# The x_proj matmuls of a Mamba-like block as two column tiles of one PSUM bank

## The chip, the core and the metric

The kernel runs on one core of a Trainium2 chip. The metric is the device time of one execution in microseconds (us), lower is better. All arithmetic is fp32.

## What is computed

The input x has shape (8, 384, 32, 32). Two layers follow one another, each with a group norm ahead of it and x added behind it. The first is a state-space (Mamba) block with an MLP, the second a mixture of four experts of which two are weighted per pixel. Cut to what matters here, the first layer is:

```python
t = layernorm(t)                                # (8, 1024, 384)
xm, z = split(t @ in_proj_w.T)                  # 768 channels each
xc = silu(causal_conv3(xm) + conv_b)
dbc = xc @ x_proj_w.T                           # 768 -> 24 + 16 + 16
dt, Bm, Cm = split(dbc, [24, 40])
dt = softplus(dt @ dt_proj_w.T + dt_proj_b)
h[l] = exp(dt * A) * h[l-1] + dt * xc * Bm      # 16 states per channel
y = (sum(h * Cm) + xc * D) * silu(z)
t = y @ out_proj_w.T;  t = gelu(t @ w1.T + b1) @ w2.T + b2
```

`dbc`, the product of `xc` with `x_proj_w`, is what the change is about: 56 numbers per token out of 768.

## The kernel before

Tokens are cut into 16 chunks (`NCH`) of 512 (`T`), two for each of the eight images. Channels lie on the 128 partitions: 384 are three blocks (`J`), 768 are six (`ND`). The 16 states are worked on as 4 steps (`NG`) of 4 states (`Q`), so a chunk takes 6 x 4 = 24 rounds, and the scan part of the kernel runs 384 rounds.

The backbone of a round is written out by hand in the loop over `rounds`: GpSimd multiplies dt * xc by B (`drive`, L738), ScalarE makes the four decays exp(dt * A) (`decay`, L730), VectorE runs four scans along the tokens (`scan`, L746), VectorE and GpSimd multiply by C (`read_out`, L750), and TensorE sums the states with four matmuls that lie beside one another in four column tiles of 32 (`sum_states`, L772). Decays, scans and read-out hand over to one another in both directions: the decays write PSUM tiles that the scans and the read-out have to leave first.

All other work is written as generators, called tasks: the next chunk's norm, input projection with convolution, gate, `x_proj` and `delta` (the dt projection), and for earlier chunks the output projection, both MLP layers and the first layer of the experts. A task yields the engine that its next step needs, a cost in us, and after how many slots it may go on. Three times in a round (`side`, a third of a round each) the engines get credit (TensorE 2.7, VectorE 0.6, ScalarE 2.7, 1.8 and 0.7), and `issue` lets the most urgent steps whose time has come go on while the credit lasts. A step that yields `"bank"` also needs one of four PSUM banks (`ps_g`), which `bank` takes and `free` gives back. All this happens while the program is built: on the chip every engine works off a fixed order, and instructions wait for one another by semaphores. A changed cost or wait of one task can therefore change the order of everything behind it. `plan` says in which round of a chunk the next chunk's tasks begin: convolutions in rounds 5 to 10, `x_proj` in round 11, the first `delta` in round 17, the loads of B and C (L374) from round 20 on.

`x_proj` (L361) is six matmuls, one for each block of 128 channels, that accumulate into 56 partitions of one bank. Each needs its block of `xc`, and these are finished in two batches of three by `silus` (L349). Then ScalarE copies the sum to SBUF (`dbc`, L366), and the SP queue writes the 32 rows of B and C to DRAM (`bc_dram`, L369), from where `load_b` and `load_c` fetch them spread over the partitions. The 24 rows of dt go into the matmul of `delta` (L399).

Ahead of the rounds, chunk 0 is prepared alone: its six convolutions with `x_proj(0)` and then its first `delta` stand in the open. After the rounds the pipeline of the MLP and the experts is drained, and the experts' second layer (L940) runs with no scan beside it.

Of the kernel before, what the change touches and what calls it, by code (L numbers as in the profile page):

```python
# [11 lines left out]
F32 = mybir.dt.float32  # L12
AF = mybir.ActivationFunctionType
ALU = mybir.AluOpType
# [4 lines left out]
P = 128  # L19
B, C, L = 8, 384, 1024  # L20
T = 512
# [4 lines left out]
ND = DI // P  # L26
# [11 lines left out]
DTR = 24  # L38
# [72 lines left out]
def layers(ctx, tc, io, ident, cmean, eps, dram, x1_dram, gn1, logits, r_dram, group_norm):  # L111
# [6 lines left out]
    nc = tc.nc  # L118
    V, S, G, PE = nc.vector, nc.scalar, nc.gpsimd, nc.tensor

    def pool(name, bufs, stack=ctx, **kw):
        return stack.enter_context(tc.tile_pool(name=name, bufs=bufs, **kw))
# [6 lines left out]
    p1, pdt, pxt, pdu = (pool(name, bufs, scanning)  # L129
                         for name, bufs in (("p1", 1), ("pdt", 2), ("pxt", NH), ("pdu", 3)))  # L130
# [16 lines left out]
    def weight(name, shape, queue=S):  # L147
        t = wp.tile(shape, F32, name="w_" + name)
        queue.dma_start(t, io[name])
        return t  # L150
# [5 lines left out]
    w_x = weight("x_proj", [P, ND, DTR + 2 * NS])  # L156
# [33 lines left out]
    xc, zs, dtr, dxr, dbc, bc_dram, bt, ct, gn = {}, {}, {}, {}, {}, {}, {}, {}, {}  # L190
# [8 lines left out]
    def bank(name):  # L199
        held[0] += 1  # L200
        return ps_g.tile([P, T], F32, name=name, tag="g")

    def free():
        held[0] -= 1
# [148 lines left out]
    def x_proj(i):  # L353
        g = None
        m = DTR + 2 * NS
        for d in range(ND):
            while (i, d) not in xc:
                yield "-", 0, 1
            yield "bank" if d == 0 else "PE", 1, 1 if d % 3 == 0 else 0
            g = bank("g_x") if d == 0 else g  # L360
            PE.matmul(g[0:m, :], lhsT=w_x[:, d, :], rhs=xc[i, d], start=(d == 0), stop=(d == ND - 1))  # L361
        yield "ACT", 0.6, 2
        while i > 0 and (i - 1, ND - 1) not in projected:
            yield "-", 0, 1
        dbc[i] = p1.tile([m, T], F32, name="dbc")
        S.copy(dbc[i], g[0:m, :])  # L366
        free()
        bc_dram[i] = dram.tile([2 * NS, T], F32, name=f"bc_dram{i}")
        nc.sync.dma_start(bc_dram[i], dbc[i][DTR:m, :])  # L369

    def load_rows(name, i, first):
        t = pbc.tile([P, T], F32, name=name)
# [346 lines left out]
    def at(r):  # L719
        i, k = divmod(r, per)  # L720
        return i, *divmod(k, NG)
# [75 lines left out]
    def behind_act():  # L797

        return 2 if now[0] == 2 else 1
# [23 lines left out]
    def plan(i, k):  # L823
# [8 lines left out]
        if n < NCH:  # L832
            if 5 <= k < 11:
                begin(conv(n, k - 5))
            if k in (7, 10):
                begin(silus(xc, accs, [(n, k - 7 + d) for d in range(3)]))
            if k in (11, 12, 13):
                begin(gate(n, k - 11))
            if k == 11:
                begin(x_proj(n))  # L840
            if k == 13:
                begin(silus(zs, gates, [(n, d) for d in range(3)]))
            if k == 17:
                begin(delta(n, 0), rank=0)
            if k == 21:
                begin(delta(n, 1), rank=0)
            if k >= per - NG:
                load_b(n, k - (per - NG))
            if k > per - NG:
                load_c(n, k - (per - NG) - 1)  # L850
# [97 lines left out]
    with tc.manual_schedule():  # L948
# [4 lines left out]
        drain()  # L953
        S.preload_act_table_set(SILU_SET)
        begin(*(conv(0, d, at_once=True) for d in range(ND)), x_proj(0))
        drain(lambda: len(xc) == ND)
        exp_ln_tables()
# [46 lines left out]
        for r in range(rounds):  # L1004
            i, d, s = at(r)
            k = r % per
# [74 lines left out]
```

## Time and profile before

| | us |
|---|---|
| median of 3 runs | 3979.28 (3975.89 to 3981.76) |
| the profiled execution | 3978.56 |
| its span, first to last instruction | 3976.8 |
| x_proj matmuls L361, 192 records | 97.7 busy |
| ScalarE's copy L366, 16 records | 9.2 busy, 575 ns each |
| VectorE's add from PSUM and SBUF L529, 48 records, 128x512 | 32.4 busy, 676 ns each |
| first to last round | about 72 to 3274 |
| experts' second layer, from about 3480 | 497.5 busy in L940 |

How to read it. PE is TensorE's matmul, PEld its weight load, DVE is VectorE, ACT ScalarE, POOL GpSimd, SP the queue from which most DMAs are issued. TensorE does an fp32 matmul in two passes, and the trace has a record for each: 192 records are 16 chunks of six matmuls. Passes overlap at their ends (a record lasts some 0.6 us where the next one starts 0.43 us later), so the distance from start to start is the measure of what one costs. The chain of waits is followed back from the last instruction, at each step to what released it; in a window it shows what set the pace there. A digit of the slices is the busy share of a fortieth of the span, in tenths.

### The profile page before, as it was taken

To read this page: it belongs to the slowest core of one execution; us is meant where nothing else is said; L and a number is where in the kernel's file an instruction comes from. 1 tells how busy PE (TensorE), PEld (TensorE's weight loads), DVE (VectorE), ACT (ScalarE), POOL (GpSimd) and SP (SyncE) were. 2 spreads that over 40 slices of the span, in tenths; PEclk is the share of its full clock that TensorE was granted. 3 is DMA by queue.
4 is the path that set the end of the run, shared out by engine and by line. 5 is a ranking of instruction groups with operands and counts; after the bars stand their busy time and mean duration, and the time that the engine had idled before them with its cause. 6 is when DMAs were issued, how large, how long until landed. Compare 5 with 4: busy or idle time off the path is not lost.

```text
span 3976.8 us, 35106 instructions
## 1 busy us (share of the span) xinstructions
PE 3654.0 (92%) x10294; PEld 1379.6 (35%) x10294; DVE 3029.6 (76%) x3081; ACT 2388.2 (60%) x3714; POOL 2780.9 (70%) x1070
## 2 busy tenths in 40 slices
PE   6679898999899989998999999999998998799999
PEld 2123232333333333333333333333333333344444
DVE  4988998888888888888888888888887771155554
ACT  4758676867686768676877677767777753100000
POOL 3998999788878888888888888888888870000000
PEclk8879898999999999999999999999999999899999
DMA  4444444465546554555555556554555553555552
GB/s 128 133 144 145 158 147 165 156 212 171 182 161 208 172 175 161 200 173 177 173 195 177 181 167 202 178 183 163 174 178 170 181 170 99 199 191 181 198 185 106
DMA packets 374803, 677.89 MB, mean 170 GB/s; under 512 B 40508, under 2 KB 151484, under 8 KB 372436
## 3 DMA queue, kind: packets, MB, share of 16 engines
q1 hardware_dynamic: 344800, 624.97, 47.3%
q10 hardware_dynamic: 29812, 50.68, 3.4%
q8 instruction: 82, 1.34, 0.1%
q14 instruction: 109, 0.89, 0.1%
HBM read 535.90 MB, written 139.59 MB: 170 GB/s over the span
## 4 chain that ended last, share of the span: by engine, by line
PE 58%; ACT 19%; DVE 14%; DMA 5%; issue 4%; SPq 1%; POOL 0%; ACTq 0%; DVEq 0%; POOLq 0%
PE acc L940 13%; PE acc L522 9%; PE g_in L298 8%; PE hid L483 7%; PE e_hid L618 7%; PE y L772 5%; PE g_out L461 5%; DVE da_A L746 4%; ACT da_A L730 4%; DVE du L746 4%; ACT da_B L730 2%; DMA r_dram<-r 2%; PE g_dt L399 2%; PE g_x L361 2%; ACT L194 2%
## 5 line engine op out<-in xcount | busy, mean ns | idle before, releaser
L738 POOL TENSOR_TENSOR du<-dxr,b 128x2048 f32<-128x2048 f32 x384 | 1738.7, 4528 | 29.4 <-PE y L772 18.4
L750 POOL TENSOR_TENSOR du<-du,c 128x1024 f32<-128x1024 f32 x384 | 906.3, 2360 | 235.3 <-DVE du L746 205.6
L730 ACT ACTIVATE da_B<-dtr_b,w_a_log 128x512 f32<-128x512 f32 x768 | 527.2, 686 | 404.1 <-DVE du L746 360.9
L730 ACT ACTIVATE da_A<-dtr_a,w_a_log 128x512 f32<-128x512 f32 x768 | 528.6, 688 | 245.4 <-DVE carry L755 120.2
L298 PE MATMUL g_in<-xt,in_proj 128*128 128x512 f32 x1152 | 559.4, 625 | 34.4 <-ACT edge L315 11.3
L618 PE MATMUL e_hid<-xn,e_w 128*128 128x512 f32 x1152 | 536.5, 611 | 40.9 <-DMA xn<-xn_dram 20.5
L746 DVE TENSOR_TENSOR_SCAN du<-da_B,carry,du 128x512 f32<-128x512 f32 x384 | 488.4, 1272 | 100.8 <-ACT da_B L730 100.0
L772 PE MATMUL y<-du,sel 128*32 128x512 f32 x3072 | 451.6, 631 | 120.1 <-DVE du L750 76.9
L483 PE MATMUL hid<-tt,mlp_w 128*128 128x512 f32 x1152 | 533.1, 603 | 21.0 <-ACT h L487 17.4
L522 PE MATMUL acc<-h,mlp_w 128*128 128x512 f32 x1152 | 532.1, 606 | 21.1 <-ACT h L498 10.4
L746 DVE TENSOR_TENSOR_SCAN du<-da_B,du 128x512 f32<-128x512 f32 x384 | 464.7, 1210 | 93.0 <-ACT da_B L730 73.6
L746 DVE TENSOR_TENSOR_SCAN da_A<-da_A,carry,du 128x512 f32<-128x512 f32 x384 | 490.2, 1276 | 54.7 <-ACT da_A L730 54.7
L746 DVE TENSOR_TENSOR_SCAN da_A<-da_A,du 128x512 f32<-128x512 f32 x384 | 466.8, 1216 | 60.3 <-ACT da_A L730 58.3
L940 PE MATMUL acc<-r,w_e_w 128*128 128x512 f32 x1152 | 497.5, 595 | 9.5 <-DVE r L929 9.5
L750 DVE TENSOR_TENSOR du<-da_A,c 128x1024 f32<-128x1024 f32 x384 | 470.3, 1225 | 13.2
L298 PEld LDWEIGHTS g_in<-xt,in_proj 128*128 128x128 f32 x1152 | 213.6, 196 | 376.7 <-issue 259.4
L618 PEld LDWEIGHTS e_hid<-xn,e_w 128*128 128x128 f32 x1152 | 216.5, 193 | 343.2 <-issue 268.8
L522 PEld LDWEIGHTS acc<-h,mlp_w 128*128 128x128 f32 x1152 | 216.0, 193 | 331.7 <-issue 252.6
L483 PEld LDWEIGHTS hid<-tt,mlp_w 128*128 128x128 f32 x1152 | 212.5, 190 | 317.1 <-issue 242.9
L940 PEld LDWEIGHTS acc<-r,w_e_w 128*128 128x128 f32 x1152 | 219.9, 191 | 286.5 <-issue 276.8
L461 PE MATMUL g_out<-xc,out_proj 128*128 128x512 f32 x576 | 272.3, 622 | 19.4 <-DVE xc L779 12.5
L772 PEld LDWEIGHTS y<-du,sel 128*32 128x32 f32 x3072 | 65.4, 109 | 424.1 <-issue 106.4
(125 smaller groups left out, 3011.7 us busy)
## 6 DMA issues: line engine op xcount, KB each, us to landing
dxr<-dxr_dram SPq DMA_DIRECT2D x384, 256.0 KB, 4.8
mlp_w<-in_mlp_w SPq DMA_DIRECT2D x384, 192.0 KB, 3.2
dtr_b<-dtr_dram SPq DMA_DIRECT2D x192, 256.0 KB, 4.2
dtr_a<-dtr_dram SPq DMA_DIRECT2D x192, 256.0 KB, 3.3
r_dram<-r ACTq DMA_DIRECT2D x192, 256.0 KB, 3.4
r<-r_dram SPq DMA_DIRECT2D x64, 768.0 KB, 4.6
in_proj<-in_in_proj SPq DMA_DIRECT2D x192, 192.0 KB, 3.6
e_w<-in_e_w SPq DMA_DIRECT2D x192, 192.0 KB, 3.8
```

The source lines that it names most:

```text
L194: S.preload_act_table_set(EXP_LN_SET)
L298: PE.matmul(g, lhsT=w[:, j, :], rhs=xt[i][:, j, :], start=(j == 0), stop=(j == J - 1))
L461: PE.matmul(g, lhsT=w[:, d, :], rhs=xc[i, 3 * k + d], start=(k + d == 0), stop=(k == 1 and d == 2))
L483: PE.matmul(g, lhsT=w[:, j, :], rhs=tt[i][:, j, :], start=(j == 0), stop=(j == J - 1))
L522: PE.matmul(g, lhsT=w[:, n, :], rhs=hs[mine[n]], start=(k + n == 0), stop=(k == 1 and n == 2))
L618: PE.matmul(h, lhsT=w[:, j, :], rhs=xn[:, j, :], start=(j == 0), stop=(j == J - 1))
L730: S.activation(out, dtr[i, d][pair][:, j % 2, :], AF.Exp, scale=neg_a[:, d, j, s:s + 1])
L738: G.tensor_tensor(du[r], dxr[i, d], wide(bt[i, s].unsqueeze(1), [P, Q, T]), ALU.mult)
L746: V.tensor_tensor_scan(a if j < 2 else b, a, b, start, ALU.mult, ALU.add)
L750: engine.tensor_tensor(du[r][:, js, :], h, wide(ct[i, s].unsqueeze(1), [P, 2, T]), ALU.mult)
L772: PE.matmul(y[j * m:(j + 1) * m, :], lhsT=sel, rhs=h[:, j, :], start=False, stop=(s == NG - 1), tile_position=(0, j * m), skip_group_check ...
L940: PE.matmul(acc[j], lhsT=e2[:, e, d, j, :], rhs=r[:, d, :], start=(e + d == 0), stop=(e + d == E + J - 2))
```

## The change

The six matmuls become three pairs. Block d (0 to 2) goes to the column tile at 0, which writes partitions 0 to 55, and block d + 3 to the column tile at 64, which writes partitions 64 to 119 of the same bank. Each tile accumulates its three blocks. ScalarE copies the first tile's sum to SBUF as before, and VectorE then adds the second tile's sum from PSUM to that copy. A pair waits for both its blocks of `xc`; its step costs 1.1 where a single matmul cost 1, and only the first pair waits for a slot. The bank is given back after VectorE's add, which is put one or two slots behind the copy (`behind_act()`), and the DMA to `bc_dram` is issued a slot after that.

```diff
     def x_proj(i):
         g = None
         m = DTR + 2 * NS
-        for d in range(ND):
-            while (i, d) not in xc:
+
+        for d in range(ND // 2):
+            while (i, d) not in xc or (i, d + ND // 2) not in xc:
                 yield "-", 0, 1
-            yield "bank" if d == 0 else "PE", 1, 1 if d % 3 == 0 else 0
+            yield "bank" if d == 0 else "PE", 1.1, 1 if d == 0 else 0
             g = bank("g_x") if d == 0 else g
-            PE.matmul(g[0:m, :], lhsT=w_x[:, d, :], rhs=xc[i, d], start=(d == 0), stop=(d == ND - 1))
+            for k in range(2):
+                PE.matmul(g[k * P // 2:k * P // 2 + m, :], lhsT=w_x[:, k * ND // 2 + d, :], rhs=xc[i, k * ND // 2 + d],
+                          start=(d == 0), stop=(d == ND // 2 - 1), tile_position=(0, k * P // 2))
         yield "ACT", 0.6, 2
         while i > 0 and (i - 1, ND - 1) not in projected:
             yield "-", 0, 1
-        dbc[i] = p1.tile([m, T], F32, name="dbc")
-        S.copy(dbc[i], g[0:m, :])
+        sums = p1.tile([m, T], F32, name="dbc")
+        S.copy(sums, g[0:m, :])
+        yield "DVE", 0.75, behind_act()
+        V.tensor_tensor(sums, g[P // 2:P // 2 + m, :], sums, ALU.add)
         free()
+        yield "-", 0, 1
         bc_dram[i] = dram.tile([2 * NS, T], F32, name=f"bc_dram{i}")
-        nc.sync.dma_start(bc_dram[i], dbc[i][DTR:m, :])
+        nc.sync.dma_start(bc_dram[i], sums[DTR:m, :])
+        dbc[i] = sums
```

The helper that it calls:

```python
    def behind_act():
        return 2 if now[0] == 2 else 1
```

## The prediction

> **What bounds the kernel now.** First the page's busy line and its 40 slices, to see which engine is full and where.
>
> ```profile
> PE 3654.0 (92%) x10294; PEld 1379.6 (35%) x10294; DVE 3029.6 (76%) x3081; ACT 2388.2 (60%) x3714; POOL 2780.9 (70%) x1070
> PE   6679898999899989998999999999998998799999
> DVE  4988998888888888888888888888887771155554
> POOL 3998999788878888888888888888888870000000
> ```
>
> TensorE is fullest, but over the first six slices VectorE and GpSimd are as full. x_proj runs only in the scan part, so the second view is busy time per chunk of 24 rounds (columns: window, length, PE, PEld, DVE, ACT, POOL, granted clock, DMA share, GB/s).
>
> ```profile
> 72.00:256.00 184.00, 112.74 (x297) 30.92 (x298) 160.65 (x171) 117.13 (x183) 172.93 (x77) 0.74 0.43 140
> 256.00:446.00 190.00, 168.16 (x484) 57.62 (x486) 171.08 (x157) 137.62 (x213) 172.08 (x57) 0.91 0.45 147
> 446.00:632.00 186.00, 164.24 (x480) 56.74 (x472) 168.98 (x184) 136.06 (x208) 174.66 (x77) 0.93 0.49 161
> 840.00:1044.00 204.00, 195.50 (x570) 72.06 (x568) 171.22 (x186) 145.54 (x221) 175.82 (x78) 0.98 0.56 187
> 1044.00:1248.00 204.00, 191.90 (x573) 70.91 (x574) 172.07 (x158) 152.52 (x243) 171.77 (x56) 0.97 0.52 171
> ```
>
> Chunks 0 to 2 leave TensorE idle for 22 us and more; GpSimd bounds them. From chunk 3 on, expert work joins, a chunk takes 202 to 208 us, TensorE idles some 10 of them, VectorE and GpSimd about 30. Third, inside such a chunk, the chain of waits around x_proj (start, us, what):
>
> ```profile
> 942.38 2.84 PE g_in L298 x6
> 945.22 2.71 PE g_x L361 x6
> 947.93 2.77 PE hid L483 x6
> 950.71 2.57 PE e_hid L618 x6
> 953.28 1.00 PE y L772 x8
> 954.28 2.79 PE acc L522 x6
> ...
> 970.92 1.00 PE y L772 x8
> 971.91 2.71 PE g_x L361 x6
> 974.63 2.77 PE acc L522 x6
> ...
> 995.24 1.00 PE y L772 x8
> 996.23 1.07 PE g_dt L399 x2
> ...
> 997.37 0.70 ACT dt L403
> ```
>
> From 942 to 996 the chain is TensorE almost without a break, and both halves of x_proj lie in it. A record is one pass; an fp32 matmul is two. Six passes after a run of the same form take 2.57 us (0.43 each); after a change of form 2.77. The eight passes of y (four column tiles of 32, two passes each) take 1.00 us, hardly more than two passes in a row: tiles run side by side. Last, the same chain in a chunk of the other parity:
>
> ```profile
> 1176.49 1.00 PE g_x L361 x2
> 1180.26 0.99 PE g_x L361 x2
> 1182.24 1.85 PE g_x L361 x4
> 1185.09 1.00 PE g_x L361 x2
> ```
>
> With the piece at 1169.15 (0.99 us) that is x_proj in five pieces, each paying its own entry.
>
> **What the Trainium skill says.** "TensorEngine Tiling (Array Packing)", Tiling Modes: a 128-row array splits into two tiles of 128x64 that work independently, and a change of mode drains the engine. The trace agrees as far as it goes: y shows four tiles at once, and entering g_x (56 columns) already costs a little (2.71 for six passes against 2.57), so it seems to run in the narrow mode today. No run shows two 64-wide tiles together. "PSUM — Partial Sum Buffer", Specifications: a VectorE instruction takes at most one tensor from PSUM; hence the copy by ScalarE first. "VectorE: DVE Perf Modes", the errata section, prices an fp32 tensor_tensor of 512 at 691 ns; the nearest row, the add of L529 from PSUM and SBUF, shows 676 ns, and I use that.
>
> **TensorE, removed.** Six matmuls of two passes become three pairs. By y, a pair costs what one matmul does, so x_proj costs one run of six passes: 2.71 us. In chunks like 840 to 1044 it was 2 x 2.71, and the run at 945 also made the next one 2.77 where 2.57 would do; the one at 971 stands behind y, where the follower pays anyway. Saving 2.71 + 0.20 = 2.9 us. In the other parity it was 0.99 + 1.00 + 0.99 + 1.85 + 1.00 = 5.83; saving 3.1. Mean 3.0 at full clock, 3.06 at the 0.98 of these windows. Twelve chunks (3 to 14) hold an x_proj and are bound by TensorE: 12 x 3.06 = 36.7 us. In chunks 0 to 2 I count nothing: GpSimd covers it.
>
> **How much of it arrives.** From 943 to 996 TensorE is busy 52.16 of 53.00 us, VectorE 44.82, GpSimd 44.96, ScalarE 38.45. So the others can come forward about 8 us before one of them is full, more than the 3 asked. But from 996 to 1044 TensorE is busy only 42.18 of 48.00: there the chain passes through ScalarE (dt, decays) and VectorE (scans), and part of an early arrival turns into waiting. Bounds: nothing arrives, or all. I take three quarters, 27.5 us, since the stretch with x_proj is bound by TensorE for 54 us and what follows is released by its last matmul (g_dt releases dt at 997).
>
> **VectorE, added.** One add per chunk, 0.68 us, plus a wait on the copy: the comparable steps behind ScalarE (dt of L409, xc of L317) idle 42.4 and 52.0 us over 96 instructions, 0.4 to 0.5 us each. So 1.1 us per chunk. In chunks 3 to 14 it lies in VectorE's 30 us of idle: nothing, unless it lands directly ahead of a scan that ScalarE waits for (da_B waits 360.9 us for du, the largest wait of all). In chunks 0 to 2 GpSimd is the bound but the scans feed it: 0.5 each, 1.5 us. Behind the waiting add stand the scans, and behind them the decays and GpSimd's read-out: up to 4 us per chunk if the copy sits behind a batch of Silu or Gelu (two table loads of 1.28 and three activations of 0.62).
>
> **Moved.** The first pair needs xc of blocks 0 and 3, so the half that ran in round 12 goes to the time of the second half, round 16. The bank of g_x is then held from the first pair to the add, some 10 us, where it was held from 945.22 to the copy that ends at 976.7, about 31 us, one bank of four. That can only help TensorE find a bank: 0 to 10 us in total, not counted. dbc is complete one or two thirds of a round later (3 to 6 us). Its DMA to bc_dram is issued a third later still, past whatever SP holds there; SP waited for the copy 9 times, 38.8 us, which should shrink. Who needs dbc: g_dt at 996.16, 20 us after the copy at 976.17, covered. In chunks 1 and 2 it follows the copy within about a microsecond, but its delta is used only at the next chunk, some 45 us on. The rows of b are loaded from round 20, 40 us on. Without that cover the delay would cost 3 to 6 us per chunk.
>
> **Chunk 0's own x_proj** stands in the open: copy at 54.99, DMA at 55.59, g_dt at 55.62. The last pair ends no later than the last matmul did, and ScalarE's table load ends at 54.97 anyway; the add comes on top: +0.75 us with its handover.
>
> **Sum.** -27.5 + 1.5 + 0.75 = -25 us against the profiled execution's 3978.56 (span 3976.8, so 1.8 lie around it): 3953.5. The median of the runs is 3979.28, 0.7 above; I give 3954.
>
> **Rivals.**
> *Absorbed.* TensorE finishes early, and rounds 18 to 23 give it back to ScalarE and VectorE. For it: the 5.8 us of idle from 996 to 1044. Against it: 8 us of room on every other engine in the stretch before. Time 3979 - 0 to 8, say 3976.
> *Pairs don't overlap.* Twelve passes in a single run, 5.3 us, save 0.1 to 0.5 per chunk, 5 in all, less 2.25 for the add: 3976. Against it: y.
> *Slower: the add holds the ring of scans and decays.* If ScalarE's copy is late behind a table batch, the add stops VectorE for about 4 us plus its own 0.68; the ring, not TensorE, then sets the chunk. Net 4.7 - 3.0 = 1.7 us over 15 chunks: 25 us, 4004. It decides once the copy runs later than the third or two that the add is put behind it. For it: the longest waits of such steps are 6 to 7 us (6.8 for xc, 6.0 for dt). Against it: the mean is 0.5. The order of all work behind x_proj is worked out anew from the changed costs, so such a meeting can't be excluded.
>
> **Numbers.** Forecast 0.62, own range 3938 (all 36.7 and a little from the bank) to 3968; absorbed 0.12; no overlap 0.05; slower 0.21. Range for 8 in 10: 3930 to 3995, which leaves out the worst of the slower case. What can be told from no change is about 0.2%, 8 us. Faster: the forecast and a sliver of the absorbed, 0.63; within 8 us: 0.16; slower 0.21.
>
> **What would show it.** Right: g_x as one run of twelve records in about 2.7 us, pairs starting some 10 ns apart; chunks 3 to 14 each 2 to 3 us shorter; TensorE idle per chunk hardly grown; the add with under 1 us of idle before it. Wrong: g_x records 0.43 us apart; chunks unchanged with TensorE idle up by 3; or VectorE's idle ahead of the add at several us, and da_B's wait for du grown.

## The result, and the profile after

The changed kernel takes 4020.12 us (median of 4 runs) against 3978.21 for the one before: a ratio of 1.0112, with a 95% interval of 1.0100 to 1.0123. It is 42 us slower, where 25 us faster was forecast and the range ended at 3995.

The page of the kernel after: its span, the busy line, and the slices of TensorE, VectorE and GpSimd.

```profile
span 4018.4 us, 35165 instructions
PE 3643.2 (91%) x10294; PEld 1384.9 (34%) x10294; DVE 3041.5 (76%) x3097; ACT 2387.2 (59%) x3714; POOL 2782.3 (69%) x1070
PE   6679888999899989998999899999999999799999
DVE  4988998888887888788888888887878881155544
POOL 3998998788978888788788888888888980000000
```

TensorE's busy time fell by only 11 us, although x_proj alone gave back 47. The groups of the kernel after say that the change itself did what it should (line, engine, operation, tiles | busy us, mean ns | idle before, by releaser):

```profile
L363 PE MATMUL g_x<-xc,w_x_proj 128*56 128x512 f32 x192 | 50.3, 619 | 1.2 <-ACT xc L322 1.2
L371 DVE TENSOR_TENSOR dbc<-g_x,dbc 56x512 f32<-56x512 f32 x16 | 11.1, 694 | 3.5 <-ACT dbc L369 3.0
```

x_proj's matmuls went from 97.7 to 50.3 us, and the add waits 3.5 us in all its 16 instances. TensorE's timeline in one chunk (start, us, line, operation, idle before in brackets) shows the pairs as one run:

```profile
1183.88 1.06 PE L588 MATMUL g_logits<-x,w_gate_w 128*32 128x512 f32 x6
1184.87 2.79 PE L363 MATMUL g_x<-xc,w_x_proj 128*56 128x512 f32 x12
1187.59 2.84 PE L529 MATMUL acc<-h,mlp_w 128*128 128x512 f32 x6
```

Twelve passes from 1184.87 to the next start at 1187.59: 2.72 us, as forecast. (As whole matmuls in the same order, in one of the kernels below, they take 5.29.)

So where did the time go? The windows of chunks 3 to 14 as one stretch, first before, then after (window, length, PE, PEld, DVE, ACT, POOL, granted clock, DMA share, GB/s):

```profile
632.00:3077.00 2445.00, 2316.07 (x6846) 855.56 (x6846) 2058.61 (x2046) 1786.53 (x2778) 2085.95 (x793) 0.98 0.54 178
```

```profile
633.00:3121.00 2488.00, 2312.51 (x6846) 860.48 (x6846) 2067.21 (x2057) 1785.52 (x2778) 2086.81 (x793) 0.96 0.53 175
```

These twelve chunks account for 43 us, all of the loss. TensorE's idle time grew from 128.9 to 175.5 us (length less busy), by 46.6. Its busy time fell by 3.6 with the same number of passes. x_proj's own busy time there fell from 70.5 to 33.5 us, by 37.0, so the other passes took some 33 us longer: the granted clock, the share of its full speed that TensorE is given, fell from 0.98 to 0.96.

One wait makes the growth of the idle time. TensorE's timeline at the start of a chunk, before:

```profile
848.63 2.74 PE L618 MATMUL e_hid<-xn,e_w 128*128 128x512 f32 x6
851.30 1.06 PE L772 MATMUL y<-du,sel 128*32 128x512 f32 x8
852.30 5.42 PE L461 MATMUL g_out<-xc,out_proj 128*128 128x512 f32 x12
...
877.89 2.84 PE L298 MATMUL g_in<-xt,in_proj 128*128 128x512 f32 x6
880.57 2.74 PE L618 MATMUL e_hid<-xn,e_w 128*128 128x512 f32 x6
```

and after:

```profile
849.28 2.74 PE L625 MATMUL e_hid<-xn,e_w 128*128 128x512 f32 x6
851.95 1.06 PE L779 MATMUL y<-du,sel 128*32 128x512 f32 x8
861.04 7.66 PE L625 MATMUL e_hid<-xn,e_w 128*128 128x512 f32 x12 [8.03 <-DMA xn<-xn_dram]
868.53 2.74 PE L468 MATMUL g_out<-xc,out_proj 128*128 128x512 f32 x6
```

`e_hid` is the experts' first layer, a task that x_proj has nothing to do with. It works through the input `xn` of one chunk, then loads that of the next into the same single buffer (`pxn` has one), so the load can't begin before the last matmul on the old one has ended. Before, 36 passes of the output projection and more stand between that matmul and the first on the new `xn`: 29 us from 851.30 to 880.57, about 25 of them full-speed work by the count of passes. After, only the eight passes of y do: TensorE stands for 8 us until the data is there. Then twelve passes take 7.66 us, where the twelve of the output projection in the lines of before take 5.42. Two windows, from within the wait to behind those passes, give a granted clock of 0.50 and then of 1.00 (columns as above):

```profile
855.40:865.50 10.10, 4.46 (x6) 1.88 (x7) 10.03 (x10) 3.64 (x6) 9.49 (x6) 0.50 0.55 207
865.60:872.00 6.40, 6.40 (x22) 2.37 (x20) 1.24 (x3) 2.07 (x3) 0.44 (x1) 1.00 0.43 146
```

That is what the Trainium skill describes in "TensorE: Matmul & The Clock Gate", Part 1: an engine that stood idle over a window of about 3.4 us is put to half its clock and gets the full one back only after a busy window. The trace agrees in kind, with a wide spread: at six such waits the clock halves 2.3 to 5.2 us after the last pass and is full again 2.9 to 5.3 us after the passes resume. The rows of the waits for `xn` in the whole of the kernel before, in the whole of the one after, and in its chunks 3 to 14 (engine and line, awaited: us in total, times, longest):

```profile
PE e_hid L618 <- DMA xn<-xn_dram: 20.5, 3, 13.8
```

```profile
PE e_hid L625 <- DMA xn<-xn_dram: 66.1, 8, 12.9
```

```profile
PE e_hid L625 <- DMA xn<-xn_dram: 49.5, 6, 8.6
```

It happens at six places in the scan part, in every second chunk from chunk 4 on; the other two of the eight waits lie near the end of the rounds and behind it, where the kernel before has them too. In chunks 3 to 14 the kernel before has none, and 49.5 us is a little more than the whole growth of the idle time: other waits shrank. Of the slower passes less is owed to it. Behind the six waits the half clock lasts 25.6 us in all, which costs about 13 us of work; the other 20 of the 33 us lie elsewhere in the twelve chunks, where the clock is also at half more often than before. The chain of waits after shows how the load starts (what the chain followed, with its times):

```profile
853.63 0.56 SPq L219
...
854.30 6.70 DMA xn<-xn_dram
...
861.04 7.66 PE e_hid L625 x12
868.70 2.58 PE g_out L468 x6
```

The last matmul on the old `xn` ends at 852.01, and the load is issued at 854.25: up to then the SP queue issues other loads that stand ahead of it. So here its place in the queue sets its start, and not the single buffer; no run gave `xn` a second buffer or issued its load earlier.

### The profile page after: what moved, and what is told of

Its sections match the earlier page's. It is cut to its first block, busy times and chain, and to the rows that moved or that the text cites. A ratio compares the mean times of both kernels' runs of the same rounds, so it can differ in the third digit from the quotient of the medians.

```text
span 4018.4 us, 35165 instructions
## 1 busy us (share of the span) xinstructions
PE 3643.2 (91%) x10294; PEld 1384.9 (34%) x10294; DVE 3041.5 (76%) x3097; ACT 2387.2 (59%) x3714; POOL 2782.3 (69%) x1070
## 4 chain that ended last, share of the span: by engine, by line
PE 57%; ACT 19%; DVE 13%; DMA 5%; issue 4%; SPq 1%; POOL 1%; ACTq 0%; DVEq 0%; POOLq 0%
PE acc L947 12%; PE acc L529 9%; PE g_in L298 8%; PE e_hid L625 7%; PE hid L490 6%; PE g_out L468 5%; PE y L779 5%; DVE da_A L753 4%; ACT da_A L737 4%; DVE du L753 4%; ACT da_B L737 3%; ACT L194 2%; PE g_dt L406 2%; DVE du L757 2%; ACT h L505 2%
## 5 line engine op out<-in xcount | busy, mean ns | idle before, releaser
L625 PE MATMUL e_hid<-xn,e_w 128*128 128x512 f32 x1152 | 554.5, 627 | 88.4 <-DMA xn<-xn_dram 66.1
L629 ACT ACTIVATE r<-e_hid,w_e_b 128x512 f32<-128x512 f32 x192 | 130.0, 677 | 155.5 <-PE e_hid L625 116.4
```

The lines of the kernel that those rows point to most:

```text
L625: PE.matmul(h, lhsT=w[:, j, :], rhs=xn[:, j, :], start=(j == 0), stop=(j == J - 1))
L629: S.activation(r, h, AF.Relu, bias=e_b1[:, u:u + 1])
```

## The experiments

The theory: the instructions of the change save what they should, but the lower cost that x_proj declares moves other tasks in the fixed order, and the expert task comes to stand straight behind its load. The rivals: VectorE's add holds the ring of scans and decays, or the tiles are not worth what the trace of before lets one think. Kernels of one group share their runs of the kernel before (medians 3975.9, 3979.0, 3975.5, 3974.7 and 3981.7).

**Making and unmaking the wait by one number outside x_proj.** The number is the slots that the expert task waits behind its load.

```diff
         nc.sync.dma_start(xn, xn_dram[i])
-        yield "-", 0, 3
+        yield "-", 0, 4
```

In the changed kernel, four slots:

> The changed kernel with one number changed outside x_proj: the expert task waits four slots behind the load of xn where it waited three, which puts 25 us of other TensorE work between the last expert matmul of a chunk and the first of the next, as in the kernel before (the changed kernel has 1 us there). Theory (order): 3940 to 3965 us. Rival (add or tiling): about 4015.

3956.8 us, ratio 0.9952 (0.9935 to 0.9969). Five slots:

> The changed kernel with five slots behind the load of xn: 28 us of other work between. Theory: no wait for xn, 3945 to 3970 us, by chance of the order better or worse than with four.

3959.0 us, 0.9946 (0.9932 to 0.9961). In the kernel before, two slots instead of three, with x_proj untouched:

> The kernel before, untouched in x_proj, with the expert task waiting two slots behind the load of xn where it waited three. That alone puts the first expert matmul of every second chunk straight behind the load (1 us of other TensorE work between, where there were 25). Theory (the wait for xn and the clock that it costs make the changed kernel slow): six waits of about 8 us plus the half clock behind each, 4015 to 4050 us. Rival (something in the new x_proj): stays within 10 us of 3976.

4034.7 us, 1.0141 (1.0126 to 1.0156). Its timeline shows the same picture, though here the profile puts the wait down to "issue" and not to the load:

```profile
852.96 2.74 PE L618 MATMUL e_hid<-xn,e_w 128*128 128x512 f32 x6
855.63 1.06 PE L772 MATMUL y<-du,sel 128*32 128x512 f32 x8
863.94 7.84 PE L618 MATMUL e_hid<-xn,e_w 128*128 128x512 f32 x12 [7.24 <-issue]
```

The load lands at 863.85, just ahead of these passes. So the order alone makes the old kernel slower than the changed one, and the changed kernel without that order is faster than the old. The control, four slots in the kernel before:

> Control: the kernel before with four slots behind the load. 28 us of other TensorE work lie between, so no wait for xn, as before. Theory: within 12 us of 3976, so that what the changed kernel gained with four slots is not due to the four slots themselves. Rival (four slots are simply a better order): 3955 or less.

3964.6 us, 0.9963 (0.9950 to 0.9977): at the edge of the theory's range. Four slots are worth some 14 us by themselves, and none of it lies in chunks 3 to 14 (2447 us from y to y, 2445 before): the last chunk takes 193 us instead of 201, and what follows its last y takes 683 instead of 692. So only part of the gain at four slots is owed to the tiles.

**Same order, other instructions.** The order of the changed kernel with whole matmuls and no add, so that nothing but the tiles and the add differ:

```diff
             for k in range(2):
-                PE.matmul(g[k * P // 2:k * P // 2 + m, :], lhsT=w_x[:, k * ND // 2 + d, :], rhs=xc[i, k * ND // 2 + d],
-                          start=(d == 0), stop=(d == ND // 2 - 1), tile_position=(0, k * P // 2))
+                PE.matmul(g[0:m, :], lhsT=w_x[:, k * ND // 2 + d, :], rhs=xc[i, k * ND // 2 + d],
+                          start=(d + k == 0), stop=(d + k == ND // 2))
...
         yield "DVE", 0.75, behind_act()
-        V.tensor_tensor(sums, g[P // 2:P // 2 + m, :], sums, ALU.add)
```

> The order of the changed kernel with the instructions of the one before: at each of the three steps two whole matmuls follow one another into the first 56 partitions, and there is no add (its yield stays). Theory (order): the wait for xn stays and TensorE's saving is gone, 4030 to 4060 us. Rival (add or tiling): back at 3978.

4051.5 us, 1.0190 (1.0167 to 1.0213). The same with four slots:

> The order of the changed kernel with four slots, with six whole matmuls and no add. Against the same order with pairs (3957) it shows what the column tiles are worth where nothing waits for xn. Theory: 3980 to 3995, that is 25 to 35 us for the tiles. Rival (the tiles are worth little once the wait is gone): 3957 to 3970.

3986.7 us, 1.0017 (1.0006 to 1.0029). Against the pairs in the same orders (ratios 1.0112 and 0.9952) the tiles, less the add, are worth 0.78% and 0.65% of 3978: 31 us with the wait and 26 without it, each uncertain by 8 to 10.

The wait is not all that the new order costs. With four slots, whole matmuls and no add, the order of the changed kernel comes to 1.0017 and that of the kernel before, the control, to 0.9963. That is 21 us, uncertain by 7, where neither waits for `xn` in chunks 3 to 14. Of the 75 us that the new order costs with three slots (1.0190), some 54 would then go with the wait, if four slots are worth the same in both orders. What makes the other 21 wasn't followed up; in the traces of the two, the clock is at half for 160 us of chunks 3 to 14 and for 119.

**The add.** The changed kernel without it, its yield kept:

> The changed kernel without VectorE's add, its yield kept, so the order of all else is the same; the second tile's sum is left out of dbc. Theory (order): the add lies in VectorE's idle time, 4010 to 4020 us. Rival (the add holds up the ring of scans and decays): 3995 or less.

4021.8 us, 1.0122 (1.0095 to 1.0148): no gain. Where the change puts the add, it costs nothing that these runs can tell; the two intervals leave some 11 us open, and an order without the wait was not tried this way.

**The pairs in the order of the kernel before.** The six steps and their costs stay; the first three issue nothing and the last three a pair each:

```diff
             yield "bank" if d == 0 else "PE", 1, 1 if d % 3 == 0 else 0
             g = bank("g_x") if d == 0 else g
-            PE.matmul(g[0:m, :], lhsT=w_x[:, d, :], rhs=xc[i, d], start=(d == 0), stop=(d == ND - 1))
+            for k in range(2 if d >= ND // 2 else 0):
+                e = d - ND // 2
+                PE.matmul(g[k * P // 2:k * P // 2 + m, :], lhsT=w_x[:, k * ND // 2 + e, :], rhs=xc[i, k * ND // 2 + e],
+                          start=(e == 0), stop=(e == ND // 2 - 1), tile_position=(0, k * P // 2))
...
         S.copy(dbc[i], g[0:m, :])
+        V.tensor_tensor(dbc[i], g[P // 2:P // 2 + m, :], dbc[i], ALU.add)
```

> The three pairs and VectorE's add, but put into the yields of the kernel before (six steps of cost 1, nothing issued in the first three, a pair in each of the last three, the add straight behind the copy), so that all other work stands in the order of the kernel before. Theory (what costs is the new order: from chunk 3 on the first expert matmul of every second chunk comes straight behind the load of its xn): no such wait, TensorE's saving arrives, 3940 to 3960 us. Rival (the add or the tiling themselves cost): 3995 or more.

3971.7 us, 0.9983 (0.9973 to 0.9993). A miss: no wait for `xn`, and yet hardly a gain. I first took it that TensorE's saving is given back to waits in this order. Against that, the add taken away:

> The pairs in the order of the kernel before, without VectorE's add; the second tile's sum is left out of dbc. With the add that kernel came to 0.9983 of the one before, where 0.990 to 0.995 was expected. Theory (TensorE's saving in the old order is given back to waits in rounds 13 to 18): 3966 to 3974. Rival (the add, which stands straight behind the copy there and waits for it 16.9 us in all, holds up the scans): 3958 or less.

3947.2 us, 0.9927 (0.9908 to 0.9946). That theory fell, and the rival stood: here the add costs 22 us (0.9983 less 0.9927), uncertain by 9. Chunks 3 to 14 take 2412 us without it, 33 less than in the kernel before. Its row in the first of the two kernels says how:

```profile
L370 DVE TENSOR_TENSOR dbc<-g_x,dbc 56x512 f32<-56x512 f32 x16 | 11.1, 693 | 17.1 <-ACT dbc L369 16.9
```

Straight behind the copy it waits 17.1 us where the changed kernel's waits 3.5, and the scans stand behind it in VectorE's queue. The same with the add one slot later (and the bank given back behind it; 5 of 5052 places in TensorE's order differ):

> The pairs in the steps of the kernel before, with the add one slot behind the copy and the bank given back behind the add (which shifts the order of a few other steps a little). Theory (the add's place cost, not the add): 3942 to 3955. Rival (the add itself costs, wherever it stands): 3965 to 3975.

3956.0 us, 0.9945 (0.9927 to 0.9963), just above the theory's range: its wait is 3.5 us again, and 15 of the 22 us are back. The other 7 are the add itself, the slightly different order or noise; these runs don't part them.

**Which part of the diff moves the expert task.** The cost of a pair alone, so that x_proj takes as much of TensorE's credit as before:

```diff
-            yield "bank" if d == 0 else "PE", 1.1, 1 if d == 0 else 0
+            yield "bank" if d == 0 else "PE", 2, 1 if d == 0 else 0
```

> The changed kernel with a cost of 2 for each pair where it had 1.1, so that x_proj takes 6 of TensorE's credit as in the kernel before; the instructions are the same. In the built program 25 us of other work then lie between the last expert matmul of a chunk and the first of the next again. Theory (the freed credit let the expert task run up to the load): no wait for xn, 3935 to 3965. Rival (the bank taken later, or the pairs in one run, bring the slow order): about 4020.

3940.4 us, 0.9904 (0.9879 to 0.9929), with the output projection back between the two expert matmuls:

```profile
848.46 2.74 PE L625 MATMUL e_hid<-xn,e_w 128*128 128x512 f32 x6
851.13 1.06 PE L779 MATMUL y<-du,sel 128*32 128x512 f32 x8
852.12 5.42 PE L468 MATMUL g_out<-xc,out_proj 128*128 128x512 f32 x12
...
878.65 2.74 PE L625 MATMUL e_hid<-xn,e_w 128*128 128x512 f32 x6
```

Its chunks 3 to 14 in one stretch:

```profile
633.00:3043.00 2410.00, 2284.25 (x6846) 854.04 (x6846) 2065.23 (x2058) 1786.38 (x2778) 2085.57 (x794) 0.97 0.54 181
```

2410 us against 2445 before: the stretch is 35 us shorter. All instructions of the change are in this kernel; only a number that steers the order differs from the changed kernel. Its order comes near that of the kernel before but isn't the same: x_proj apart, 265 of 5052 places in TensorE's order differ, where the changed kernel differs in 1526.

**Other versions.** The pairs in the old order, add straight behind the copy, four slots:

> The pairs in the order of the kernel before with four slots behind the load of xn (that order with whole matmuls: 3965). If the old order takes only a few us of the saving, 3955 to 3963; if the saving arrives whole, 3930 to 3940.

3951.2 us, 0.9930 (0.9912 to 0.9948), between the two. The changed kernel with six and with nine slots:

> The changed kernel with six slots behind the load: 34 us of other work between, no wait for xn. Theory: 3945 to 3970, like four and five.

> The changed kernel with nine slots behind the load: 20 to 41 us of other work between, no wait for xn. Theory: 3945 to 3975; later than needed, so the experts may end later.

3938.4 us, 0.9906 (0.9885 to 0.9926), below the expected range, and 3986.3 us, 1.0024 (1.0016 to 1.0033). The second is a miss: no wait for `xn`, yet slower than before. The kernel before with six slots:

> The kernel before with six slots behind the load of xn. If the best version owes its time to the tiles (about 35 us), 3960 to 3985; if to the six slots, 3935 to 3950.

4006.9 us, 1.0077 (1.0059 to 1.0095): slower than with three, against both expectations, so the six slots don't explain the 3938. Last, the add one slot later in the old steps with six slots:

> The pairs in the steps of the kernel before, the add one slot behind the copy, six slots behind the load of xn. Theory: no wait for xn (30 us or more of other work), the saving arrives, 3930 to 3955.

3939.2 us, 0.9908 (0.9891 to 0.9925). The three best, 3938 to 3940, can't be told apart; they beat the kernel before by about 37 us and the changed one by 80. Why nine slots, or six in the kernel before, are slow wasn't followed up. A trace shows only where TensorE stands: with six slots in the kernel before, `hid` and `e_hid` wait some 85 us for ScalarE's `h` (L487), and 30 with three.

## Why the prediction was wrong, by its own steps

**What bounds the kernel: right.** Chunks 3 to 14 are bound by TensorE. What it gains or loses there, the kernel gains or loses.

**TensorE, removed: right.** 36.7 us were worked out, and x_proj's busy time in chunks 3 to 14 fell by 37.0. The pairs overlap, so that rival is out: what the Trainium skill says of two 128x64 tiles ("TensorEngine Tiling (Array Packing)", Tiling Modes), open in the trace of before, is seen here as twelve passes in 2.72 us.

**How much arrives: not refuted, perhaps low.** Three quarters were taken, 27.5 us. Between kernels of the same order the tiles are worth 26 and 31 us, which fits. In single profiles the twelve chunks became 33 us shorter in the order of the kernel before without the add, and 35 with the cost of 2, which would be nearly all; but the second has other differences in its order.

**VectorE, added: right for the place where the change puts it.** The add took 694 ns where 676 were taken and waits 0.2 us on average where 0.4 were taken, and leaving it out gains nothing that the runs can tell. The "slower" rival, the add that holds the ring of scans, did not occur; but its mechanism is real, as the old-order kernel with the add straight behind the copy showed (22 us; the rival's price was 25).

**Moved: here it failed.** The step followed x_proj's own instructions, and those of its neighbours that need `dbc` or the bank, and found each of them covered. It held that a freed bank "can only help TensorE", and counted nothing for the credit: 3.3 where 6 were taken. That credit is what let the expert task issue a step earlier and go on to the next chunk ahead of the output projection, with its load still under way. The slots that the program gives to each step show how, in the same way at all six places. The expert task's last step in a chunk goes out in the second third of round 23 and not in the last. The three slots behind its load then end in the second third of round 0, where the output projection becomes ready only in the last. TensorE's credit is full, and two expert steps go out, straight behind the load. With the cost of 2, or with four slots, the expert task becomes ready in the last third of round 0 again, and the output projection, more urgent, goes first. The order of other tasks was named, under the rivals, as something that could meet the add; the load of `xn` was never looked at. The profile of before held a hint: the wait of `e_hid` for `xn`, shown above (20.5 us), is the largest that TensorE has for any DMA, though its three cases lie around the end of the rounds and none in chunks 3 to 14. That the new order costs 21 us even without this wait was not counted either.

**The sum.** The 36.7 us went away as forecast, 37 by measure. TensorE's idle time grew by 46.6 us, which the new wait makes, and the other passes took some 33 us more, of which about 13 stand behind that wait. 46.6 + 33 - 37 = 43, the growth of the stretch; the 33 is what is left of the busy time, so the sum has to close. The same instructions in an order without the wait come near the forecast of 3954: 3940 with the cost of 2, and 3957 with four slots, which are worth some 14 us by themselves.

## What to carry to other kernels

Where the order of work is made from declared costs, a cost is part of the change: price the instructions and the new order apart, and check which loads lose the work that covered them. To know which of the two a result comes from, run the new instructions in the old order and the old instructions in the new one. If a knob is turned to take a wait away, turn it in the old kernel too: four slots were worth 14 us there. And an add that waits for another engine should stand far enough behind what it waits for that the queue it stands in need not wait with it: one slot made 15 us here.

## What I had not expected of the hardware

How much of the loss is not idle time. In the case shown, twelve passes behind a wait of 8 us take 2.2 us more than twelve at the full clock. Over the twelve chunks the passes other than x_proj took some 33 us more, against 46.6 us of new idle time; about 13 of the 33 stand right behind the six waits, and the cause of the other 20 stays open.
